# Key norms from the diagonal of k kᵀ, and triangular substitution on GpSimd, in a gated delta-rule block

## The chip, the cores and the metric

One core of one Trainium2 chip. The metric is the device time of one execution in microseconds (us); the median of three runs is compared.

## The reference, cut to what matters

The program is one adaptive-layernorm block: a linear-attention layer with a gated delta rule, then a sparse feed-forward layer, for 8 sequences of 256 tokens and 256 channels. For each of 16 key heads (two value heads each) the attention computes, over tokens t:

```python
q = _l2norm(qkv_c[..., :QD].reshape(Bq, Tq, NK, DK))
k = _l2norm(qkv_c[..., QD:2 * QD].reshape(Bq, Tq, NK, DK))
def step(S, inp):
    Sk = jnp.einsum('bhi,bhipj->bhpj', k_t, S)
    dv = b_t[..., None] * (v_t - Sk)
    upd = jnp.einsum('bhi,bhpj->bhipj', k_t, dv)
    S = S * d_t[:, :, None, :, None] + upd
    o = jnp.einsum('bhi,bhipj->bhpj', q_t, S)
```

`qkv_c` is a projection followed by a causal convolution over four tokens. The kernel does not step through tokens. It takes chunks of 128 tokens and solves, for each, a triangular system of 128 x 128 whose matrix holds the products k kᵀ scaled by decays, betas and the squared norms of the keys.

## The kernel before, in words

All of it is float32. Sequences go in pairs (`bp`, four pairs), key heads in groups of four (`kh`, `GH = 4`), so there are 16 groups and 64 combinations of pair and head. A head has two sequences x two chunks (`NCH = 2`) x two value heads, eight triangular systems; a group has 32, and each is cut into four diagonal blocks of 32 x 32 (`Q = 32`), 128 blocks in all, one per partition.

While a group is attended to, the next one is made ready (`ahead`), in these steps.

- `stage_a`, once per head: project the keys (`ps_k`, L432), convolve them (ScalarE L418, VectorE L420) into `k_t`. `norms2` then transposes `k_t` on TensorE (`ps_n2k`, L447, four transposes) and lets ScalarE square and sum each of the four pieces (L451, `junk`). From the squared norms VectorE makes `rk2` (L505) and `bk` (L507), and GpSimd the tile `diag` (L516) and `nk` (L523). TensorE forms k kᵀ (`ps_kk`, L532), VectorE runs a scan with decays over `diag` (`e`, L551; L547 in the first group) and multiplies `ps_kk` with `e` into `a_t` (L563). Four DMAs on the SP queue store the diagonal blocks to `scr` (L572).
- `stage_b`, once per group: load the 128 blocks (`blk`, L585), write the diagonal (GpSimd memset, L587), and invert them all at once by substitution, 30 steps of two VectorE instructions, a product into `tmp` (L604) and a subtraction from `blk` (L610). A step handles j x (31 - j) elements per partition, 30 to 240. After half of the steps and again at the end `turn` has ScalarE write negated copies (L592, L597); at the end they are stored to `scr_x` and `scr_y`.
- `levels`, once per head: load pieces of those inverses (`x_even`, `moved`, `x_top`, `low_up`) and join them on TensorE to 64 x 64 and then 128 x 128 (`ps_w`, `ps_t`, from L709 on).

Attention proper works on one head at a time: `prepare` makes q, v and the output gate (`cv`, `gz`), `attend` applies the inverses and ends with the output's norm on GpSimd (`rs`, a power, L105) and the gating on VectorE (`og`, L873), and `shares` multiplies with the output weights (`ps_y`, L903). Feed-forward and input normalisation of other sequences run in between (`feed_forward`, `fill`).

Generators are interleaved by `along`, which also paces the next group's preparation. The final order on every engine is made by the framework's scheduler at build time from its own estimate of durations; each engine then runs its instructions strictly in that order. PSUM is split in three pools: `ps_in` (three banks), `ps_inv` (two, with `ps_kk`, the levels and feed-forward) and `ps_mix` (three). In the first group no attention is there to run beside: `first_solved` holds the first heads' attention behind the substitution.

Of the kernel before, what the change touches and what calls it, by code (L numbers as in the profile page):

```python
# [11 lines left out]
F32 = mybir.dt.float32  # L12
AF = mybir.ActivationFunctionType
ALU = mybir.AluOpType
AX = mybir.AxisListType
# [3 lines left out]
P = 128  # L19
# [29 lines left out]
def adaln_block(  # L49
# [18 lines left out]
    nc = tc.nc  # L68
# [4 lines left out]
    NCH = T // P  # L73
    NK = w_heads.shape[0]
    NV = 2 * NK
    NS = 2 * NCH
# [6 lines left out]
    small = ctx.enter_context(tc.tile_pool(name="small", bufs=4))  # L83
    dram = ctx.enter_context(tc.tile_pool(name="dram", bufs=2, space=DRAM))
    ps_in = ctx.enter_context(tc.tile_pool(name="ps_in", bufs=3, space=PSUM))
    ps_inv = ctx.enter_context(tc.tile_pool(name="ps_inv", bufs=2, space=PSUM))
    ps_mix = ctx.enter_context(tc.tile_pool(name="ps_mix", bufs=3, space=PSUM))

    def bank(pool, shape, name):
        return pool.tile(shape, F32, tag=pool.name, name=name)  # L90
# [5 lines left out]
    ident = identx[:, 1:PE1]  # L96
# [269 lines left out]
    with ExitStack() as scope:  # L366
        rec_pool = scope.enter_context(tc.tile_pool(name="rec", bufs=7))
# [73 lines left out]
        def norms2(src, name):  # L441

            n2 = small.tile([P, 2, NCH], F32, tag=name, name=name)
            ps = bank(ps_in if name == "n2k" else ps_in, [P, 2, NCH, P], f"ps_{name}")
            for i in range(2):
                for n in range(NCH):
                    nc.tensor.transpose(ps[:, i, n, :], src[:, i, n * P : (n + 1) * P], ident)  # L447
            for i in range(2):
                for n in range(NCH):
                    junk = mixp.tile([P, P], F32, tag="junk", name="junk", bufs=2)  # L450
                    nc.scalar.activation(  # L451
                        junk, ps[:, i, n, :], AF.Square, accum_out=n2[:, i, n : n + 1]
                    )
            return n2
# [24 lines left out]
        def stage_a(kh, bp, hp, wk, h_bp, scr):  # L479

            rec = {"kh": kh, "bp": bp, "hp": hp, "h": h_bp}
            first = bp == 0 and kh < GH
            if not first:
                dbc = single.tile([P, 2, NS * PE1], F32, tag="dbc", name="dbc")
                nc.sync.dma_start(
                    out=dbc,
                    in_=d_dram[bp][kh]
# [3 lines left out]
            k_t = rec_pool.tile([P, 2, T], F32, tag="k_t", name="k_t")  # L491
# [4 lines left out]
            else:  # L496
                convolved(k_t, ps, conv_sb[:, kh, 0, :])
            yield rec
            n2 = norms2(k_t, "n2k")
            nc.vector.tensor_scalar_max(n2, n2, L2_EPS2)  # L500
            nk = small.tile([P, 2 * NCH], F32, tag="nk", name="nk", bufs=7)
            rec["nk"] = nk
# [5 lines left out]
                out=bk,  # L508
                in0=beta[bp][:, :, 2 * kh : 2 * kh + 2],
                in1=rk2[:, :, None].to_broadcast([P, 2 * NCH, 2]),  # L510
                op=ALU.mult,
# [13 lines left out]

            e = rec_pool.tile([P, 2, NS, PE1], F32, tag="e", name="e")
            rec["e"] = e
            ps_kk = bank(ps_inv, [P, 2 * NCH, P], "ps_kk")
            for i in range(2):
                for n in range(NCH):  # L530
                    kc = k_t[:, i, n * P : (n + 1) * P]
                    nc.tensor.matmul(ps_kk[:, i * NCH + n, :], lhsT=kc, rhs=kc, start=True, stop=True)  # L532
            if first:
                e_f, diag_f = e.rearrange("p i s t -> p (i s t)"), diag.rearrange("p s t -> p (s t)")
                for c0 in range(0, 2 * NS, 3):
# [21 lines left out]
                    ALU.add,  # L557
                )
            yield rec
            a_t = rec_pool.tile([P, 2, NS, P], F32, tag="a_t", name="a_t", bufs=6)  # L560
            rec["a"] = a_t
            for i in range(2):
                nc.vector.tensor_tensor(  # L563
                    out=a_t[:, i].rearrange("p (n h) t -> p n h t", h=2),
                    in0=ps_kk[:, i * NCH : (i + 1) * NCH, None, :].to_broadcast([P, NCH, 2, P]),
                    in1=e[:, i, :, 0:P].rearrange("p (n h) t -> p n h t", h=2),
                    op=ALU.mult,
                )
            a_f = a_t.rearrange("p i s t -> p (i s) t")
            scr_v = scr.rearrange("(g s q) a b -> g q a s b", g=GH, q=NQ)  # L570
            for q in range(NQ):
# [5 lines left out]
        def stage_b(scr, scr_x, scr_y):  # L577

            blk = single.tile([P, Q, Q], F32, tag="blk", name="blk")
            nc.sync.dma_start(out=blk, in_=scr)  # L585
            xb = single.tile([P, Q, Q], F32, tag="xb", name="xb")
            nc.gpsimd.memset(blk.rearrange("p a b -> p (a b)")[:, :: Q + 1], -1.0)  # L587
            yield

            def turn(rows):  # L590

                nc.scalar.activation(  # L592
                    xb[:, rows], blk[:, :, rows].rearrange("p b a -> p a b"), AF.Copy, scale=-1.0
                )
                if rows.stop == Q:
                    nc.sync.dma_start(out=scr_x, in_=xb)
                nc.scalar.activation(blk[:, :, rows], blk[:, :, rows], AF.Copy, scale=-1.0)  # L597
                if rows.stop == Q:
                    nc.sync.dma_start(out=scr_y, in_=blk)

            for j in range(1, Q - 1):
                m = Q - 1 - j
                tmp = single.tile([P, j, m], F32, tag="tmp", name="tmp", bufs=2)
                nc.vector.tensor_tensor(  # L604
                    out=tmp,
                    in0=blk[:, j, None, j + 1 :].to_broadcast([P, j, m]),
                    in1=blk[:, 0:j, j, None].to_broadcast([P, j, m]),
                    op=ALU.mult,
                )
                solved = nc.vector.tensor_tensor(  # L610
                    out=blk[:, 0:j, j + 1 :], in0=blk[:, 0:j, j + 1 :], in1=tmp, op=ALU.subtract
                )
                yield solved.ins
                if j == Q // 2:
                    turn(slice(0, Q // 2))
            turn(slice(Q // 2, Q))
            yield
# [599 lines left out]
```

## Time and profile before

| | |
|---|---|
| median of three runs | 2112.94 us (2111.67 to 2115.77) |
| profiled execution | 2109.53 us, span 2107.7 us |
| mean granted TensorE clock | 0.992 |
| DMA packets | 231.10 MB, mean 110 GB/s |

A row of the groups reads: line, engine, operation, output<-inputs, form x count | busy us in all, mean ns of one | idle time of the engine just before them and what ended most of it. A row of the timeline reads: start us, duration us, engine, line, operation, and in brackets the idle time before it. PE is TensorE, DVE VectorE, ACT ScalarE, POOL GpSimd, SPq the DMA queue of SyncE. TensorE shows two records for one float32 product and one for a transpose; the ends of its records are modelled.

### The profile page before, as it was taken

The page shows a single profiled execution, that of the slowest core. Times are in us where ns is not written, and L with a number is a line of the kernel's source. Part 1 is how long each engine was busy: PE and PEld are TensorE (multiplying, and loading weights), DVE is VectorE, ACT ScalarE, POOL GpSimd, SP SyncE. Part 2 cuts the span into 40 slices and gives each one's busy share as a digit, 9 for nine tenths or more (in the row PEclk, how much of TensorE's full clock was granted, in tenths as well). Part 3 has the DMA queues.
Part 4 walks back from the last instruction along what each step waited for, and adds up shares of the span by engine and source line. Part 5 has one row for each costly group of instructions (what it writes and reads, how often), then busy time and mean ns, then how long its engine had stood idle before and what let it go on. Part 6 is the DMA issues. An engine that isn't in the chain of part 4 may idle for free.

```text
span 2107.7 us, 46922 instructions
## 1 busy us (share of the span) xinstructions
PE 2027.1 (96%) x16684; PEld 1592.2 (76%) x16684; DVE 1683.9 (80%) x4103; ACT 1314.1 (62%) x4516; POOL 368.5 (17%) x375
## 2 busy tenths in 40 slices
PE   8989999999999999999999999999999999999998
PEld 5567777777778777787777778777777877778887
DVE  6788786887889797888878788897878978788557
ACT  3567676766756666576666656667565656657652
POOL 3111312112020211213021121211202021121010
PEclk9999999999999999999999999999999999999999
DMA  4352424324343443533433454343434343343236
GB/s 134 85 131 68 117 61 108 97 71 112 82 124 97 127 113 95 141 108 106 141 87 105 112 136 117 102 116 100 124 102 122 99 125 106 102 122 107 72 92 218
DMA packets 363434, 231.10 MB, mean 110 GB/s; under 512 B 293433, under 2 KB 305081, under 8 KB 363201
## 3 DMA queue, kind: packets, MB, share of 16 engines
q1 hardware_dynamic: 343328, 167.56, 30.6%
q10 hardware_dynamic: 19872, 60.54, 9.1%
q8 instruction: 133, 2.18, 0.4%
q14 instruction: 101, 0.82, 0.1%
HBM read 188.38 MB, written 29.12 MB: 103 GB/s over the span
## 4 chain that ended last, share of the span: by engine, by line
PE 49%; DVE 25%; ACT 8%; DMA 7%; issue 6%; POOL 4%; SPq 2%; ACTq 0%; DVEq 0%; POOLq 0%
PE ps_qv L432 7%; PE ps_y L903 6%; PE ps_z L646 6%; DVE cv L420 5%; PE ps_ks L814 3%; PE ps_k L432 3%; PE ps_ff L190 3%; POOL diag L516 3%; DVE a_t L563 2%; DVE e L551 2%; DVE tmp L604 2%; DVE blk L610 2%; PE ps_out L244 2%; PE ps_o L855 2%; DVE og L873 2%
## 5 line engine op out<-in xcount | busy, mean ns | idle before, releaser
L420 DVE SCALAR_TENSOR_TENSOR cv<-ps_qv,conv_sb,cv 128x510 f32<-128x510 f32 (+2 forms) x564 | 408.2, 738 | 76.0 <-ACT cv L418 72.1
L432 PE MATMUL ps_qv<-h_bp,wh 128*128 128x512 f32 x768 | 362.8, 600 | 5.0 <-DVE cv L420 4.7
L105 POOL TENSOR_TENSOR rs<-ss,minus_halves 128x4 f32<-128x4 f32 x128 | 133.1, 1045 | 987.4 <-DVE ss L860 976.7
L646 PE MATMUL ps_z<-wh,h_bp 128*128 128x256 f32 x1024 | 255.2, 388 | 14.7 <-DVE cv L420 14.4
L903 PE MATMUL ps_y<-wo,og_p 128*128 128x256 f32 x1024 | 238.6, 381 | 1.9 <-ACT gz L653 1.4
L840 ACT ACTIVATE junk<-o 128x128 f32<-128x128 f32 x512 | 154.1, 303 | 136.8 <-DVE o L856 119.3
L432 PEld LDWEIGHTS ps_qv<-h_bp,wh 128*128 128x128 f32 x768 | 134.5, 192 | 114.8 <-issue 101.5
L646 PEld LDWEIGHTS ps_z<-wh,h_bp 128*128 128x128 f32 x1024 | 186.2, 194 | 43.2 <-DVE cv L420 18.6
L903 PEld LDWEIGHTS ps_y<-wo,og_p 128*128 128x128 f32 x1024 | 188.3, 191 | 28.4 <-issue 4.3
L604 DVE TENSOR_TENSOR tmp<-blk 128x30 f32<-128x30 f32 (+14 forms) x480 | 157.3, 328 | 47.7 <-DMA blk<-scr 39.1
L418 ACT ACTIVATE cv<-ps_qv,conv_sb 128x512 f32<-128x512 f32 x188 | 129.5, 690 | 100.4 <-PE ps_qv L432 99.9
L516 POOL TENSOR_TENSOR diag<-consts,bk 128x1032 f32<-128x1032 f32 x64 | 122.8, 1919 | 343.4 <-DVE bk L507 327.1
L551 DVE TENSOR_TENSOR_SCAN e<-dbc,diag 128x1032 f32<-128x1032 f32 x60 | 138.2, 2304 | 35.4 <-POOL diag L516 30.9
L610 DVE TENSOR_TENSOR blk<-blk,tmp 128x30 f32<-128x30 f32 (+14 forms) x480 | 157.4, 328 | 11.2
L420 DVE SCALAR_TENSOR_TENSOR k_t<-ps_k,conv_sb,k_t 128x510 f32<-128x510 f32 (+1 forms) x189 | 139.7, 741 | 26.4 <-ACT k_t L418 23.0
L873 DVE SCALAR_TENSOR_TENSOR og<-o,rs,gz 128x128 f32<-128x128 f32 x512 | 147.2, 348 | 12.4 <-POOL rs L105 10.6
L814 PE MATMUL ps_ks<-u,cross 128*128 128x128 f32 x1024 | 143.8, 280 | 1.9 <-ACT u L808 1.3
L780 ACT ACTIVATE vn<-ps_v,nk 128x256 f32<-128x256 f32 x256 | 105.7, 481 | 49.2 <-PE ps_v L775 48.9
L190 PE MATMUL ps_ff<-h,w_ff 128*128 128x128 f32 x1024 | 130.5, 277 | 3.3 <-ACT h L149 2.4
L814 PEld LDWEIGHTS ps_ks<-u,cross 128*128 128x128 f32 x1024 | 128.1, 191 | 6.9 <-ACT u L808 2.6
L190 PEld LDWEIGHTS ps_ff<-h,w_ff 128*128 128x128 f32 x1024 | 123.0, 192 | 12.0 <-issue 5.1
L432 PE MATMUL ps_k<-h_bp,wk 128*128 128x512 f32 x256 | 126.1, 613 | 2.0 <-ACT junk L451 1.2
(180 smaller groups left out, 4273.0 us busy)
## 6 DMA issues: line engine op xcount, KB each, us to landing
wh<-in_w_heads ACTq DMA_DIRECT2D x64, 640.0 KB, 4.4
w_ff<-in_w_ff SPq DMA_DIRECT2D x128, 256.0 KB, 3.1
dbc<-d_dram SPq DMA_DIRECT2D x60, 516.0 KB, 3.8
wo<-in_w_heads ACTq DMA_DIRECT2D x32, 512.0 KB, 3.8
w_dn<-in_w_down SPq DMA_DIRECT2D x64, 256.0 KB, 2.8
wk<-in_w_keys SPq DMA_DIRECT2D x16, 512.0 KB, 4.5
scr<-a_t SPq DMA_DIRECT2D x256, 32.0 KB, 2.2
blk<-scr SPq DMA_DIRECT2D x16, 512.0 KB, 4.1
```

The source lines that it names most:

```text
L190: nc.tensor.matmul(ps[:, a, l, :], lhsT=w[:, k, l, :], rhs=h2[:, k, :], start=(k == 0), stop=(k == CC - 1),)
L420: nc.vector.scalar_tensor_tensor(out=dst[:, :, d:], in0=ps[:, :, : T - d], scalar=taps[:, KC - 1 - d : KC - d], in1=dst[:, :, d:], op0=ALU ...
L432: nc.tensor.matmul(ps.rearrange("p b t -> p (b t)"), lhsT=w[k], rhs=h_bp[:, k, :], start=(k == 0), stop=(k == CC - 1),)
L516: done = nc.gpsimd.tensor_tensor(out=diag, in0=identx[:, None, :].to_broadcast([P, 2 * NS, PE1]), in1=bk.rearrange("p n h -> p (n h)")[:, ...
L551: nc.vector.tensor_tensor_scan(e.rearrange("p i s t -> p (i s t)"), dbc.rearrange("p i f -> p (i f)"), diag.rearrange("p s t -> p (s t)"), ...
L604: nc.vector.tensor_tensor(out=tmp, in0=blk[:, j, None, j + 1 :].to_broadcast([P, j, m]), in1=blk[:, 0:j, j, None].to_broadcast([P, j, m]), ...
L610: solved = nc.vector.tensor_tensor(out=blk[:, 0:j, j + 1 :], in0=blk[:, 0:j, j + 1 :], in1=tmp, op=ALU.subtract)
L646: nc.tensor.matmul(ps[:, n, :], lhsT=h_bp[:, k, i * T + n * P : i * T + (n + 1) * P], rhs=wh[:, k * 640 + 384 : (k + 1) * 640], start=(k = ...
L814: nc.tensor.matmul(ps_ks[:, ct, h, :], lhsT=cross[:, h, ct, :], rhs=u0[:, h, :], start=True, stop=True)
L840: nc.scalar.activation(junk, o[:, n, h, :], AF.Square, accum_out=ss[:, n, h : h + 1])
L873: nc.vector.scalar_tensor_tensor(out=og[:, n, h, :], in0=o[:, n, h, :], scalar=rs[:, 2 * n + h : 2 * n + h + 1], in1=gz[:, i, n, h, :], op ...
L903: nc.tensor.matmul(ps_y[:, n, :], lhsT=og_p[:, j // 2, i, n, j % 2, :], rhs=wo[:, j // 2, j % 2, :], start=(j == 0), stop=(j == 3),)
```

## The change

The squared norms of the keys are no longer made by transposing and squaring. k kᵀ is formed before them, ScalarE copies it to SBUF (into one half of `a_t`), VectorE multiplies it with the identity into the other half and sums along the rows. The products with `e` read the SBUF copy. And the 60 instructions of the substitution are issued on GpSimd instead of VectorE. Lines after the first hunk are up to 16 higher than before, L510 and L513 are the new product and sum, L609 and L615 the substitution.

```diff
@@ stage_a
-            n2 = norms2(k_t, "n2k")
+            ps_kk = bank(ps_inv, [P, 2 * NCH, P], "ps_kk")
+            for i in range(2):
+                for n in range(NCH):
+                    kc = k_t[:, i, n * P : (n + 1) * P]
+                    nc.tensor.matmul(ps_kk[:, i * NCH + n, :], lhsT=kc, rhs=kc, start=True, stop=True)
+            a_t = rec_pool.tile([P, 2, NS, P], F32, tag="a_t", name="a_t", bufs=6)
+            rec["a"] = a_t
+            a_h = a_t.rearrange("p i (n h) t -> p (i n) h t", h=2)
+            kk, diagonal = a_h[:, :, 1], a_h[:, :, 0]
+            nc.scalar.copy(kk, ps_kk)
+            n2 = small.tile([P, 2, NCH], F32, tag="n2k", name="n2k")
+            nc.vector.tensor_tensor(
+                out=diagonal, in0=kk, in1=ident[:, None, :].to_broadcast([P, 2 * NCH, P]), op=ALU.mult
+            )
+            nc.vector.tensor_reduce(
+                out=n2.rearrange("p i n -> p (i n)"), in_=diagonal, axis=AX.X, op=ALU.add
+            )
             nc.vector.tensor_scalar_max(n2, n2, L2_EPS2)
...
-            ps_kk = bank(ps_inv, [P, 2 * NCH, P], "ps_kk")
-            for i in range(2):
-                for n in range(NCH):
-                    kc = k_t[:, i, n * P : (n + 1) * P]
-                    nc.tensor.matmul(ps_kk[:, i * NCH + n, :], lhsT=kc, rhs=kc, start=True, stop=True)
...
-            a_t = rec_pool.tile([P, 2, NS, P], F32, tag="a_t", name="a_t", bufs=6)
-            rec["a"] = a_t
-            for i in range(2):
-                nc.vector.tensor_tensor(
-                    out=a_t[:, i].rearrange("p (n h) t -> p n h t", h=2),
-                    in0=ps_kk[:, i * NCH : (i + 1) * NCH, None, :].to_broadcast([P, NCH, 2, P]),
-                    in1=e[:, i, :, 0:P].rearrange("p (n h) t -> p n h t", h=2),
-                    op=ALU.mult,
-                )
+            e_h = e[:, :, :, 0:P].rearrange("p i (n h) t -> p (i n) h t", h=2)
+            for h in range(2):
+                nc.vector.tensor_tensor(out=a_h[:, :, h], in0=kk, in1=e_h[:, :, h], op=ALU.mult)
@@ stage_b
             for j in range(1, Q - 1):
                 m = Q - 1 - j
                 tmp = single.tile([P, j, m], F32, tag="tmp", name="tmp", bufs=2)
-                nc.vector.tensor_tensor(
+                nc.gpsimd.tensor_tensor(
                     out=tmp,
                     in0=blk[:, j, None, j + 1 :].to_broadcast([P, j, m]),
                     in1=blk[:, 0:j, j, None].to_broadcast([P, j, m]),
                     op=ALU.mult,
                 )
-                solved = nc.vector.tensor_tensor(
+                solved = nc.gpsimd.tensor_tensor(
                     out=blk[:, 0:j, j + 1 :], in0=blk[:, 0:j, j + 1 :], in1=tmp, op=ALU.subtract
                 )
```

## The prediction

> **What bounds the kernel now.** I read the page's header and chain first, then the groups by form, then stretches of the timeline, then the busy times by window.
>
> ```profile
> span 2107.7 us, 46922 instructions
> PE 2027.1 (96%) x16684; PEld 1592.2 (76%) x16684; DVE 1683.9 (80%) x4103; ACT 1314.1 (62%) x4516; POOL 368.5 (17%) x375
> PE 49%; DVE 25%; ACT 8%; DMA 7%; issue 6%; POOL 4%; SPq 2%; ACTq 0%; DVEq 0%; POOLq 0%
> ```
>
> TensorE is busy nearly always, and half of the chain that ended last is its own work. A quarter is VectorE. So work taken off TensorE should count almost in full, and work taken off VectorE only where TensorE waits for it. The windows of one group of heads (the substitution runs from 885 to 927) say how much that can be:
>
> ```profile
> core 0: us, PE busy (x) PEld busy (x) DVE busy (x) ACT busy (x) POOL busy (x), PEclk, DMA share, GB/s
> 885.00:927.00 42.00, 40.51 (x328) 33.19 (x327) 39.67 (x123) 25.47 (x88) 5.81 (x8) 1.00 0.39 115
> 927.00:1009.00 82.00, 80.63 (x699) 62.95 (x698) 63.64 (x126) 53.13 (x190) 16.23 (x14) 1.00 0.42 112
> ```
>
> While the substitution is on it VectorE is full (39.67 of 42 us), yet TensorE idles only 1.5 us there. A free VectorE can win no more than that, some 15 to 20 us over all groups. The granted clock is 1.00, so it plays no part.
>
> The substitution itself is a chain of 60 dependent steps, and TensorE comes for its result:
>
> ```profile
> 885.55 0.16 POOL L587 MEMSET blk<- 128x32 f32 x1 [13.13 <-DMA blk<-scr]
> ...
> 926.67 0.21 DVE L610 TENSOR_TENSOR blk<-blk,tmp 128x30 f32<-128x30 f32 x1
> 926.91 1.11 ACT L592 ACTIVATE xb<-blk 128x512 f32<-128x512 f32 x1 [0.54 <-DVE blk L610]
> 928.05 0.32 SPq L596 DMA_DIRECT2D scr_x<-xb  x1
> 930.68 1.76 SPq L692 DMA_DIRECT2D x_even<-scr_x  x4
> 933.39 0.21 PE L709 MATMUL ps_w<-x_even,a_t 32*32 32x32 f32 x1
> ```
>
> blk lands at 885.5, the last step ends at 926.9, and 6.5 us later TensorE starts the next group's first level, about the moment x_even lands. There is almost no slack behind this chain. It is 41 us long because VectorE does other work between its steps. This decides the case.
>
> **TensorE, part by part.** The four transposes of L447 for the key norm go (64 heads, 256 transposes). The four products k k^T stay and only move ahead. What a head's transposes occupy is read from start to start, since the modelled ends overlap:
>
> ```profile
> 92.18 0.66 PE L447 MATMUL ps_n2k<-consts,k_t 128*128 128x128 f32 x4
> 92.67 1.05 PE L532 MATMUL ps_kk<-k_t 128*128 128x128 f32 x8
> ```
>
> That is 0.49 us; elsewhere 0.43 to 0.49. I take 0.46 x 64 = **-29 us** (27 to 31), in full, because nothing else fills TensorE's place.
>
> **ScalarE, VectorE and GpSimd.** The rows that price these:
>
> ```profile
> L451 ACT ACTIVATE junk<-ps_n2k 128x128 f32<-128x128 f32 x256 | 69.3, 293 | 33.7 <-PE ps_n2k L447 32.9
> L563 DVE TENSOR_TENSOR a_t<-ps_kk,e 128x512 f32<-128x512 f32 x128 | 82.0, 682 | 0.2
> L516 POOL TENSOR_TENSOR diag<-consts,bk 128x1032 f32<-128x1032 f32 x64 | 122.8, 1919 | 343.4 <-DVE bk L507 327.1 <-DVE mv L132 10.0 <-DVE rstd L134 6.3
> L1014 POOL TENSOR_TENSOR taps<-consts,conv_sb 128x512 f32<-128x512 f32 x1 | 1.0, 1041 | 4.6 <-DMA conv_sb<-in_conv_w 4.6
> L657 POOL TENSOR_SCALAR eps_q<-n2q 128x4 f32<-128x4 f32 x64 | 23.8, 373 | 40.4 <-ACT junk L451 36.7
> ```
>
> ScalarE loses 256 squares (69.3 us) and their accumulator reads (56.7 us), and gains 64 copies of 128x512 at 0.60 us (the copy raw, L466): 39 us. Net -87 us, off the path.
>
> VectorE loses both substitution groups (157.3 and 157.4 us) and gains a masking product and a sum per head. For both I take the 128x512 row of L563, 0.68 us (a sum reads one operand less; L131, 256 elements with one input, costs 0.42 us as products of 256 do). 64 x 1.36 = 87 us. The two a_t products keep their size. Net -228 us: VectorE falls to about 1456 us (69%). Outside the substitution windows it rises from 64 to about 69 of 82 us, still with room. The new steps lie on the way from k to diag, but that way runs a whole group ahead. They also free the ps_kk bank after the copy rather than after a_t. I book 0 for all of this, between -10 us (TensorE's idle time in the substitution windows above) and +10 us (5.4 us more VectorE work per group outside them; should an eighth of it reach the path, 15 x 0.7).
>
> GpSimd gains 960 dependent products. Two rows of its products give 1.69 ns per element ((1919 - 1041) / 520) and 0.18 us fixed. The 30 shapes average 165 elements: 0.28 + 0.18 = 0.46 us. The steps wait for one another; from the end of bk (L507) to the start of diag, GpSimd takes 0.14 us to wake. Bounds per step: 0.46 us (no waking) and 0.79 us (the fixed part of L657, 0.37, with 0.14). I take 0.46 + 0.14 = **0.59 us**, since the products' own line is nearer than another instruction's. VectorE's step was 0.33 us.
>
> **First group.** Nothing interleaves there: VectorE's chain took 23.2 us (59.8 to 83.0), and TensorE started the first level at 90.0, when x_even had just landed. On GpSimd it is 60 x 0.59 + 2 rstd at 0.65 + one eps_q = 37 us, 14 us longer. The changed kernel as built has two more ps_k projections ahead of that level (4 products of 0.86 us = 3.4 us), so **+10.5 us** (+3 at 0.46 us, +23 at 0.79).
>
> **The other 15 groups.** GpSimd's queue runs in order. In the changed kernel as built, some four rs (L105, 1.05 us each) and two eps_q stand between the chain's steps, behind each rs the og of VectorE, and behind the chain's end ScalarE's xb with the attention's copies queued after it; on SP the stores of scr_x and scr_y wait for that xb as they do now, with x_even, moved and w_ff behind them. Chain: 35.4 + 4.2 + 0.7 = 40.3 us. VectorE and GpSimd also block each other:
>
> ```profile
> 124.41 1.92 POOL L516 TENSOR_TENSOR diag<-consts,bk 128x1032 f32<-128x1032 f32 x1
> 124.79 2.47 DVE L873 SCALAR_TENSOR_TENSOR og<-o,rs,gz 128x128 f32<-128x128 f32 x4
> ```
>
> Four og take 1.12 us elsewhere (at 159.35); here the first had to wait for diag to end. No VectorE instruction with two SBUF operands gets through while diag runs, whereas cv and aq, with one operand in PSUM, keep their 0.74 and 0.68 us. About 30 such instructions fall into one substitution window. Each waits at most for the running step: 30 x 0.25 = 7.5 us of VectorE per group, covered by the 20 us it gives up there. In the other direction the trace shows little: diag took 1.95 instead of 1.92 us where VectorE had begun first. That gives 30 x 0.03 = 1 us; if GpSimd had to sit out a whole og (0.35 us) less its waking time, 30 x 0.21 = 6 us. I add 3: **43.5 us**.
>
> The allowance: adding up TensorE's rows, the built order places about 86 us of TensorE work between a group's last ps_k and the first level, where it was 78. But k k^T of the fourth head stands about 5 us later than its transposes did, and copy, product and sum take 1.5 us more than the squares. So some 1.5 us is left on top of 41.3: **43 us**. The chain is 0.5 us late per group, 15 x 0.5 = **+8 us**.
>
> Sum against the profiled execution (2109.5 us, span 2107.7): 2109.5 - 29 + 10.5 + 8 = 2099. The median of the runs (2112.9) lies 3.4 us above that execution, so 2102.
>
> **Two rules of the Trainium skill speak against the change.** "GPSIMD Engine Reference", section Performance versus the Vector engine, gives about 2.6 cycles per element at 1.2 GHz for a product of two tensors, and tells one to use VectorE; the rows here have 1.69 ns. As an estimate by that page a step is 0.08 us dearer (165 elements), a chain 4.8 us, and the time would be near 2180 us. "SBUF — State Buffer", section Who interferes with whom, says that the later of the two engines waits for the other's whole instruction; the og row agrees for VectorE, the 0.03 us of diag does not for GpSimd. As an estimate by that page the chain loses the 6 us per group rather than 3, and the time would be near 2147 us.
>
> **Rivals.**
> - *The chain on GpSimd comes late in every group* and takes the place of TensorE's transposes. For it: x_even lands just in time today, and short strided rows were never run on GpSimd here. Against: the two product rows lie on one line, and the built order leaves more room. Without lateness the change wins 18.5 us; over 15 groups that is gone at 1.2 us late, a step of 0.61 us. At 0.65 us: 39 + 4.9 + 3 = 46.9, 3.9 us late, 59 us, and 14 us at the start: 2109.5 - 29 + 14 + 59 = 2153 (2157 as median). At 0.70 us about 2205. Slower.
> - *TensorE's saved time is eaten by waits of the same size*, so that nothing shows. For it: busy spans are modelled, the chain gives TensorE only 49%. Against: start to start, products follow each other without gaps. 2109 to 2117 as median.
> - *The relief is larger*: the step is near 0.46 us, no group is late, VectorE's freed time ends TensorE's waits. 2109.5 - 29 + 3 - 10 = 2074, median 2077.
>
> **Chances.** Forecast (2090 to 2108) 0.38, larger relief 0.14, no difference 0.12, late chain 0.36. A fifth of a per cent, 4 us, is about what a measurement of this kernel can tell from no change. The range reaches down to the larger relief (2077) and up to a step of 0.65 us (2157), leaving out the dearest steps.
>
> **What would show it.** Right: TensorE 29 us less busy; L615 on GpSimd starting every 0.59 us; the last L615 ending 41 to 45 us after the memset of blk; the first L714 not idle for x_even. Wrong: ScalarE's xb waiting for L615 in most groups, TensorE idle behind x_even, VectorE's og waiting for rs, or steps above 0.65 us.

## The result, and the profile after

The changed kernel takes 2200.9 us (median of four runs, 2195.1 to 2205.2) against 2112.8 us: ratio 1.0413, 95% interval 1.0386 to 1.0440, so 87 us slower. The prediction said 2102, with a range up to 2157. The profiled execution took 2205.2 us with a span of 2203.3.

First the head of the page: span, busy times with their share of the span, and the shares of the chain that ended last.

```profile
span 2203.3 us, 46030 instructions
PE 2047.4 (93%) x16428; PEld 1598.4 (73%) x16428; DVE 1565.2 (71%) x3271; ACT 1279.1 (58%) x4069; POOL 886.2 (40%) x1335
...
PE 10%; DVE 4%; POOL 3%; DMA 2%; ACT 1%; issue 1%; SPq 0%; DVEq 0%; ACTq 0%; POOLq 0%
```

The 256 transposes are gone (16684 records became 16428), yet TensorE is busy 20 us longer, and its idle time, span less busy time, nearly doubled: 2107.7 - 2027.1 = 80.6 us before, 155.9 now. The busy time grew because of the clock. Its mean is 0.974 (0.992 before); the stretches at half speed cost TensorE 56.3 us of full-speed time within the span, before 17.1. TensorE was busy for 104.1 us of these stretches, before for 32.8. Counting that at half, its work at full speed fell from 2010.7 to 1995.3 us, so the transposes did leave some 15 us less to do. Idle time (75 us more) and half clock (36 us more) ate that several times over. Between the first 55 and the last 20 us of the span, TensorE idled for 2 us or more 26 times, 78.9 us in all; before it did so twice, 4.4 us. Those few long stalls are about as long as the whole growth of its idle time. The chain now explains only a fifth of the span and no longer names a culprit, so the waits have to be read.

The table by stretch, one substitution and the rest of its group (columns as in the prediction's table: length, busy us of the engines, granted clock, DMA share, GB/s):

```profile
925.90:968.60 42.70, 39.67 (x249) 30.81 (x246) 26.27 (x58) 22.38 (x78) 35.97 (x68) 0.96 0.26 79
968.60:1057.20 88.60, 85.20 (x773) 66.96 (x772) 68.59 (x135) 56.02 (x181) 17.13 (x15) 0.98 0.47 124
```

VectorE has its free time (it is busy for 26.27 of 42.70 us), and TensorE gets nothing from it: it stands 3.0 us in the substitution, where it stood 1.5. The rest of the group, 82 us in the table before, takes 88.6.

The substitution's own timeline in that group, from the landing of `blk` to TensorE's first level:

```profile
925.88 0.16 POOL L592 MEMSET blk<- 128x32 f32 x1 [16.52 <-DMA blk<-scr]
...
968.38 0.27 POOL L615 TENSOR_TENSOR blk<-blk,tmp 128x30 f32<-128x30 f32 x1
968.68 1.11 ACT L597 ACTIVATE xb<-blk 128x512 f32<-128x512 f32 x1 [1.82 <-POOL blk L615]
...
972.84 1.74 SPq L697 DMA_DIRECT2D x_even<-scr_x  x4
...
975.35 0.21 PE L714 MATMUL ps_w<-x_even,a_t 32*32 32x32 f32 x1
```

42.8 us against 41 before, and TensorE starts the level without having stood for `x_even`. The substitution is not late here. What is late stands in the lists of waits (the waiting instruction, what it waited for: us in all, times, longest), here the rows of VectorE, TensorE and its weight loads:

```profile
DVE og L878 <- POOL rs L105: 60.5, 28, 6.9
PE ps_u L811 <- DVE aq L801: 29.0, 13, 5.2
PE ps_ks L819 <- DVE aq L801: 19.8, 9, 3.4
PEld ps_w L714 <- DMA x_even<-scr_x: 16.9, 11, 4.7
```

Before, these four were 10.6, 5.1, 0.6 and 3.4 us. Of the 26 long stalls 13, with 38.8 of the 78.9 us, waited for `aq`. One such stall in the timeline, merged from VectorE, GpSimd and TensorE:

```profile
1053.31 0.16 DVE L865 SCALAR_TENSOR_TENSOR ss<-ss,eps_q 128x4 f32<-128x4 f32 x1 [0.82 <-ACT junk L845]
...
1057.20 0.15 POOL L592 MEMSET blk<- 128x32 f32 x1 [17.03 <-DMA blk<-scr]
...
1059.06 0.36 POOL L615 TENSOR_TENSOR blk<-blk,tmp 128x84 f32<-128x84 f32 x1
1059.38 1.01 POOL L105 TENSOR_TENSOR rs<-ss,minus_halves 128x4 f32<-128x4 f32 x1
...
1060.43 1.94 DVE L878 SCALAR_TENSOR_TENSOR og<-o,rs,gz 128x128 f32<-128x128 f32 x4 [5.17 <-POOL rs L105]
...
1068.06 0.68 DVE L801 TENSOR_TENSOR aq<-ps_kq,e 128x512 f32<-128x512 f32 x1
1068.79 1.01 PE L811 MATMUL ps_u<-vn,t_inv 128*128 128x128 f32 x3 [5.24 <-DVE aq L801]
```

`ss`, the input of `rs`, is there at 1053.5. In GpSimd's order `rs` stands behind the memset, which waits for `blk` to land, and behind six instructions of the substitution; it starts 5.9 us later (3.7 us of the load, 2.2 of the six instructions). VectorE, in order too, stands 5.17 us at `og`, then catches up with what had piled up, and `aq`, which TensorE needs, comes out 5.24 us late. The table by stretch shows what the clock makes of it (the granted clock is the first number behind the busy times):

```profile
1055.00:1060.00 5.00, 5.00 (x38) 2.92 (x37) 0.26 (x1) 4.52 (x21) 2.40 (x8) 1.00 0.55 181
...
1065.00:1070.00 5.00, 1.21 (x5) 1.21 (x6) 5.00 (x11) 0.00 (x0) 4.32 (x9) 0.69 0.00 0
1070.00:1075.00 5.00, 5.00 (x39) 4.63 (x38) 4.90 (x11) 3.03 (x12) 4.45 (x8) 0.63 0.01 3
```

At full load after the stall TensorE has a mean clock of 0.63. This stall is paid for twice: once idle, once at half speed.

### The profile page after: what moved, and what is told of

Same layout as the page of the kernel before. It is cut to its first block, busy times and chain, and to the rows that moved or that the text cites. A ratio compares the mean times of both kernels' runs of the same rounds, so it can differ in the third digit from the quotient of the medians.

```text
span 2203.3 us, 46030 instructions
## 1 busy us (share of the span) xinstructions
PE 2047.4 (93%) x16428; PEld 1598.4 (73%) x16428; DVE 1565.2 (71%) x3271; ACT 1279.1 (58%) x4069; POOL 886.2 (40%) x1335
## 5 line engine op out<-in xcount | busy, mean ns | idle before, releaser
L432 PE MATMUL ps_qv<-h_bp,wh 128*128 128x512 f32 x768 | 371.7, 611 | 0.9 <-DVE y L919 0.9
L105 POOL TENSOR_TENSOR rs<-ss,minus_halves 128x4 f32<-128x4 f32 x128 | 141.9, 1113 | 434.0 <-DVE ss L865 415.6
L651 PE MATMUL ps_z<-wh,h_bp 128*128 128x256 f32 x1024 | 260.1, 393 | 13.5 <-DVE cv L420 13.3
L615 POOL TENSOR_TENSOR blk<-blk,tmp 128x30 f32<-128x30 f32 (+14 forms) x480 | 253.9, 529 | 36.1
L609 POOL TENSOR_TENSOR tmp<-blk 128x30 f32<-128x30 f32 (+14 forms) x480 | 238.5, 497 | 33.4
L878 DVE SCALAR_TENSOR_TENSOR og<-o,rs,gz 128x128 f32<-128x128 f32 x512 | 187.7, 426 | 61.6 <-POOL rs L105 60.5
L819 PE MATMUL ps_ks<-u,cross 128*128 128x128 f32 x1024 | 149.6, 288 | 24.8 <-DVE aq L801 19.8
L819 PEld LDWEIGHTS ps_ks<-u,cross 128*128 128x128 f32 x1024 | 133.1, 198 | 41.4 <-DVE aq L801 21.6
L190 PE MATMUL ps_ff<-h,w_ff 128*128 128x128 f32 x1024 | 135.5, 281 | 13.1 <-DMA w_ff<-in_w_ff 9.9
L861 DVE TENSOR_TENSOR o<-o,ps_o 128x256 f32<-128x256 f32 x128 | 52.5, 414 | 107.5 <-PE ps_o L860 100.3
```

The source lines that it names most:

```text
L105: nc.gpsimd.tensor_tensor(out=out, in0=in_, in1=minus_halves[:, :n], op=ALU.pow)
L190: nc.tensor.matmul(ps[:, a, l, :], lhsT=w[:, k, l, :], rhs=h2[:, k, :], start=(k == 0), stop=(k == CC - 1),)
L432: nc.tensor.matmul(ps.rearrange("p b t -> p (b t)"), lhsT=w[k], rhs=h_bp[:, k, :], start=(k == 0), stop=(k == CC - 1),)
L609: nc.gpsimd.tensor_tensor(out=tmp, in0=blk[:, j, None, j + 1 :].to_broadcast([P, j, m]), in1=blk[:, 0:j, j, None].to_broadcast([P, j, m]), ...
L615: solved = nc.gpsimd.tensor_tensor(out=blk[:, 0:j, j + 1 :], in0=blk[:, 0:j, j + 1 :], in1=tmp, op=ALU.subtract)
L651: nc.tensor.matmul(ps[:, n, :], lhsT=h_bp[:, k, i * T + n * P : i * T + (n + 1) * P], rhs=wh[:, k * 640 + 384 : (k + 1) * 640], start=(k = ...
```

## The experiments

My theory after the result: in-order queues that the change rearranged make a few instructions late on every engine (for the substitution's half, `rs` behind it on GpSimd), and a stretch of half clock follows most long stalls of TensorE. The rivals: the substitution's result itself is late; the engines slow each other down in SBUF; or any other written order than that of the kernel before would lose as much. "Cost" below is (ratio - 1) x 2112.8 us, each kernel against runs of the kernel before on the same chip; the changed kernel's is +87.

| run | what it is | median us | ratio, 95% | cost us |
|---|---|---|---|---|
| e1 | new norms, substitution on VectorE | 2181.5 | 1.0306 to 1.0343 | +68 |
| e2 | old norms, substitution on GpSimd | 2181.3 | 1.0304 to 1.0345 | +69 |
| e3 | changed, `rs` on VectorE | 2183.1 | 1.0288 to 1.0349 | +67 |
| e4 | e1, `rs` on VectorE | 2191.3 | 1.0347 to 1.0390 | +78 |
| e5 | before, a third scratch buffer | 2124.7 | 1.0038 to 1.0079 | +12 |
| e6 | e2, `rs` on VectorE | 2136.8 | 1.0084 to 1.0143 | +24 |
| e7 | e1 without the diagonal | 2163.2 | 1.0201 to 1.0257 | +48 |
| e8 | changed, first substitution on VectorE | 2197.3 | 1.0346 to 1.0419 | +81 |
| e9 | e1, k kᵀ read in PSUM, no copy | 2155.5 | 1.0171 to 1.0220 | +41 |
| e10 | before, k kᵀ early and copied | 2169.0 | 1.0230 to 1.0277 | +54 |
| e11 | before, k kᵀ copied | 2148.2 | 1.0117 to 1.0200 | +33 |
| e12 | before, k kᵀ early | 2122.9 | 1.0025 to 1.0062 | +9 |
| e13 | e9, first group with old norms | 2133.0 | 1.0076 to 1.0114 | +20 |
| e14 | changed, first group as before | 2183.2 | 1.0307 to 1.0354 | +70 |
| e15 | all mends together | 2126.2 | 1.0037 to 1.0079 | +12 |
| e16 | before, norms by a column of ones | 2166.7 | 1.0229 to 1.0281 | +54 |
| e17 | before, a copy that nobody reads | 2112.4 | 1.0021 to 1.0046 | +7 |
| e18 | e11 with a tile of its own | 2124.3 | 1.0079 to 1.0113 | +20 |

### The two halves, and the scale of the output's norm (e1 to e4)

e1, against the changed kernel:

```diff
-                nc.gpsimd.tensor_tensor(out=tmp, ...)
-                solved = nc.gpsimd.tensor_tensor(...)
+                nc.vector.tensor_tensor(out=tmp, ...)
+                solved = nc.vector.tensor_tensor(...)
```

> The changed kernel with the 960 substitution instructions put back on VectorE; only the norms from the diagonal are new. If all of the loss comes from the substitution on GpSimd (queue, lateness or port), the 256 transposes saved on TensorE show: 2113 - 29 = 2084 us, with 10 us either way, and og (L878) waits for rs about as little as in the kernel before (11 us). If the norms themselves are what costs (VectorE's extra product and sum, the later k k^T), this kernel lies above 2113 us, up to 2200.

e2 is the kernel before with only the last hunk of the change, the substitution on GpSimd.

> The kernel before with the substitution on GpSimd and the old norms. If the substitution is all of the loss: 2201 + 29 = 2230 us, between 2200 and 2240, with og waiting for rs 50 us or more. If the norms are the loss: about 2113 us.

e3 is the changed kernel, e4 is e1, both with a reciprocal in place of the power -1/2 (so the scale has other values; e6 and e15 below have it too):

```diff
-            rsqrt(rs, ss.rearrange("p n h -> p (n h)"))
+            nc.vector.reciprocal(rs, ss.rearrange("p n h -> p (n h)"))
```

> The changed kernel, but the norm of the output (rs) is a reciprocal on VectorE in place of the power -1/2 on GpSimd, so that no rs stands in GpSimd's queue (the values differ by that; it costs VectorE 128 x 0.17 = 22 us and takes 142 us from GpSimd). Queue theory (rs waits behind the substitution's steps and the load of blk, og holds up VectorE behind it): more than half of the loss goes, 2150 us or less, and no wait of og for rs is left. Result theory (the inverses come late; ScalarE's xb and x_even): 2185 to 2205 us, xb still waits 40 us or more. Port theory (VectorE and GpSimd block each other): 2185 to 2205 us, og still 0.42 us instead of 0.35.

> Control for the run before it: substitution on VectorE, new norms, and the same reciprocal on VectorE. Under every theory it lies within 8 us of the kernel with the new norms alone, since rs on GpSimd made og wait only 11 us in the kernel before. If it is faster by much more, moving rs is a gain of its own and the run with rs on VectorE has to be read against this one.

Each half alone costs about 69 us (2181.5 and 2181.3), both together 87: they are not additive, and the norms, which I had booked at a gain, are half of it. e2 shows the stall of the changed kernel in its plain form: in its trace TensorE stands longer than 0.6 us at `ps_u` for `aq` 11 times, 41.7 us in all, up to 5.5 us each, most of them in the same place of a group, with VectorE 3.7 to 4.9 us at `og` for `rs` ahead of them. One of them, merged from VectorE, GpSimd and TensorE; here six substitution steps alone stand between `ss` and `rs`:

```profile
791.53 0.42 DVE L860 SCALAR_TENSOR_TENSOR ss<-ss,eps_q 128x4 f32<-128x4 f32 x1
...
795.23 0.65 POOL L610 TENSOR_TENSOR blk<-blk,tmp 128x220 f32<-128x220 f32 x1
795.84 1.01 POOL L105 TENSOR_TENSOR rs<-ss,minus_halves 128x4 f32<-128x4 f32 x1
...
796.88 2.31 DVE L873 SCALAR_TENSOR_TENSOR og<-o,rs,gz 128x128 f32<-128x128 f32 x4 [4.93 <-POOL rs L105]
...
804.22 0.67 DVE L796 TENSOR_TENSOR aq<-ps_kq,e 128x512 f32<-128x512 f32 x1
804.94 1.22 PE L806 MATMUL ps_u<-vn,t_inv 128*128 128x128 f32 x4 [5.39 <-DVE aq L796]
```

But taking `rs` off GpSimd gave only 20 us in the changed kernel (e3), where I had expected 50 or more, while the same edit in e4 cost 10, where I had allowed 8. So there was more than the queue ahead of `rs`.

### Is any other order as bad? And `rs` without the new norms (e5, e6)

e5 changes one number of the kernel before:

```diff
-                    junk = mixp.tile([P, P], F32, tag="junk", name="junk", bufs=2)
+                    junk = mixp.tile([P, P], F32, tag="junk", name="junk", bufs=3)
```

> The kernel before with one number changed: the scratch of the squared norms (tag junk) gets three buffers and not two. Every instruction stays, none gets longer; but the order that is written for each engine is made from estimated durations, and it comes out different in hundreds of places on TensorE. Theory A (both halves of the change cost about 70 us because any other order than that of the kernel before leaves TensorE short gaps, and the granted clock falls after them): 2150 to 2190 us. Theory B (each half costs its 70 us by its own waits): within 12 us of the kernel before, 2100 to 2125 us.

> The kernel before with the substitution on GpSimd (old squared norms), and the scale rs as a reciprocal on VectorE and not as a power on GpSimd (the scale has other values for it). With the substitution alone on GpSimd, TensorE stood 41.7 us in 11 gaps, each for aq, and in front of each aq VectorE had stood 3.7 to 4.9 us at og for rs, which is queued on GpSimd behind the substitution; with the half clock after each gap that is about 70 us. Theory 1 (the queue in front of rs is this half's whole loss): 2105 to 2130 us. Theory 2 (VectorE slowed by GpSimd's use of SBUF, or any other order): 2160 us or more.

e5: 2124.7, 12 us, with hundreds of instructions in other places of TensorE's order. So another order can cost 12 us by itself. One control is no bound on what an order can cost; I read a cost of 12 us or less as not to be told from order, and one of 30 or more as likely to have a cause of its own. e6: 2136.8, between the ranges of its two theories; of the substitution's 69 us, 45 go when `rs` no longer stands behind it. TensorE's stalls at `ps_u` for `aq` over 0.6 us fall from 41.7 to 18.5 us, and the half-clock loss from 55 to 17 us. That shows the queue ahead of `rs` as the main loss of this half; what the other 24 us are stays open.

### Where the norms lose (e7, e9 to e12, e17, e18)

e7 leaves the diagonal out of e1:

```diff
-            nc.vector.tensor_tensor(out=diagonal, in0=kk, in1=ident..., op=ALU.mult)
-            nc.vector.tensor_reduce(out=n2, in_=diagonal, axis=AX.X, op=ALU.add)
-            nc.vector.tensor_scalar_max(n2, n2, L2_EPS2)
+            nc.vector.tensor_reduce(out=n2, in_=kk[:, :, 0:8], axis=AX.X, op=ALU.max)
+            nc.vector.tensor_scalar_max(n2, n2, 300.0)
```

> New norms with the substitution on VectorE, as in the run of the norms alone (2181 us), but without the product with the identity and its sum: the squared norm is the largest of eight columns of the copy of k k^T, held to 300 or more, so the values are others. That leaves out 1.4 us of VectorE per head (about 90 us in all) and keeps the early k k^T, its copy on ScalarE and the product of the decays from SBUF. Theory V (VectorE's 1.5 us in a row in front of aq and x_top is the loss): 2090 to 2115 us. Theory P (the place of k k^T, the copy, the buffers, or the order): 2160 us or more.

2163.2: without VectorE's 1.5 us per head 20 of the 68 us go; 48 remain. The next four separate early place, copy and transposes. e9 is e1 with

```diff
-            nc.scalar.copy(kk, ps_kk)
-                out=diagonal, in0=kk, in1=ident...
+                out=diagonal, in0=ps_kk, in1=ident...
```

and the old product of `ps_kk` with `e`.

> New norms from the diagonal, substitution on VectorE, but k k^T is not copied to SBUF: the product with the identity and the old product of the decays both read PSUM. Against the run of the norms alone (2181 us) ScalarE loses 64 copies, and the decays' product has one operand in SBUF and not two; k k^T still stands early, and its bank is held from there to the decays' product. Theory C (the copy and the product from SBUF are the loss): 2080 to 2115 us. Theory E (the early place of k k^T is the loss): 2150 to 2190. Theory T (the transposes and their squares on ScalarE are what paced this part; without them the order is worse): 2140 to 2185.

e10 is the kernel before with these lines ahead of its norms, and the decays' product from `kk`; e11 has them in the old place behind the norms; e12 has only the matmuls ahead of the norms.

```diff
+            ps_kk = bank(ps_inv, [P, 2 * NCH, P], "ps_kk")      # and its four matmuls
+            a_t = rec_pool.tile([P, 2, NS, P], F32, tag="a_t", name="a_t", bufs=6)
+            kk = a_t.rearrange("p i (n h) t -> p (i n) h t", h=2)[:, :, 1]
+            nc.scalar.copy(kk, ps_kk)
             n2 = norms2(k_t, "n2k")
```

> The kernel before with its old norms (transposes and squares), substitution on VectorE; k k^T moved ahead of the norms and copied by ScalarE into the tile of A, and the decays' product from SBUF, as the change has them. Against the kernel before that is a copy of 0.6 us per head more. Theories C and E: 2140 to 2180 us. Theory T: 2110 to 2130.

> As the last, but k k^T stays in its old place, behind the norms: only the copy, the product of the decays from SBUF and the earlier taking of the tile of A are new. Theory C: 2140 to 2180 us. Theories E and T: 2110 to 2130.

> The kernel before with one thing moved: the four matmuls of k k^T stand ahead of the old norms and not behind them; nothing is copied, and the bank is held longer. Theory E: 2140 to 2190 us. Theories C and T: 2105 to 2130.

The early place alone costs 9 us (e12, 2122.9), the copy alone 33 (e11, 2148.2), both 54 (e10, 2169.0); with the new norms and no copy it is 41 (e9, 2155.5) instead of 68. No one of the three theories fits all four: e9 lies above the range of C, e12 below that of E, and e10 and e11 above that of T. The copy's route is the dearest part, and with the old norms still in place. And the transposes, once gone, pay next to nothing: from e10 to e7, which has no transposes and squares and in their place a small maximum on VectorE, the cost falls by 6 us, not by 29, with overlapping intervals. TensorE's work at full speed, counted as above, does fall there, from 2022.0 to 1986.9 us; its idle time (113.5 to 127.0) and its half clock take most of it back.

What in the copy? e17 keeps it and reads nothing of it; e18 gives it a tile of its own, so that the tile of A is taken late again:

```diff
+            spare = mixp.tile([P, 2 * NCH, P], F32, tag="spare", name="spare", bufs=2)
+            nc.scalar.copy(spare, ps_kk)
```

> The kernel before and one thing more: behind k k^T in its old place, ScalarE copies the bank to a spare tile that nobody reads; the decays' product reads PSUM as before. If ScalarE's 64 copies of some 0.6 us, in the order of its queue, are what cost 32 us in the run with k k^T copied (2148): 2138 to 2158 us. If it is the product from SBUF or the tile of A: 2110 to 2128.

> As the run with k k^T copied in its old place (2148 us), but the copy goes to a tile of its own, and the tile of A is taken at the decays' product as in the kernel before. If the early tile of A cost the 32 us: 2110 to 2128 us. If the copy or the product from SBUF did: 2138 to 2158.

ScalarE's 64 copies cost 7 us (e17, 2112.4 against 2106.8 on that chip), not 33. With the product reading SBUF it is 20 us (e18, 2124.3, in the range that I gave for the early tile as the cause), and with the tile taken early 33 (e11). The product from SBUF has two operands there and is blocked by GpSimd's `diag`, as the prediction saw for `og`: in the changed kernel nine of 128 take 1.4 to 2.3 us, each begun while `diag` runs and ended 0.5 us after it. Its mean is 762 ns where the product from PSUM took 682, only 10 us over 128 instructions. No wait in the trace of e11 shows what the early tile does. The steps from 7 to 20 to 33 are each about as large as another order's 12 us, so I leave them unexplained.

### The first group (e8, e13, e14)

e8 gives only the first group's substitution back to VectorE.

> The changed kernel with the first group's substitution on VectorE, the fifteen others on GpSimd. The first group's chain took 36.4 us on GpSimd against 23 us on VectorE, with nothing else to do beside it, and the changed kernel was some 32 us behind at the end of its second group. If that start is a loss of its own, 2201 - 13 - 10 = 2178 us, 2170 to 2188; if another loss takes its place, 2195 to 2205 us.

2197.3, 6 us less, with overlapping intervals: though its chain takes 36.4 us instead of 23, it is hardly the start's loss. e13 is e9 with a branch, e14 the changed kernel with the same branch and the first substitution on VectorE:

```diff
+            if first:
+                n2 = norms2(k_t, "n2k")          # and k k^T behind them, as before
+            else:
                 ...                              # k k^T, its diagonal
```

> As the norms from PSUM (2155 us), but the first group's four heads keep the old norms, with k k^T behind them. In the trace of the norms from PSUM the start of the second group's substitution was 34 us late, and the end 41.5 us. Theory S (the loss is the first group's start, where nothing else fills TensorE): 2155 - 34 = 2121, 2108 to 2132 us. Theory G (every group pays): 2140 us or more.

> The changed kernel with the first group as in the kernel before: old norms, and substitution on VectorE; the fifteen others unchanged. In the changed kernel the second group's substitution began 31.9 us late, in the run with only the first substitution on VectorE 22.5 us late. Theory S: 2201 - 25 = 2176 us, 2165 to 2185. If another loss takes its place, as in the run with only the first substitution on VectorE (2197): 2190 us or more.

e13 (2133.0, a little above what I expected) takes 21 us off e9, e14 (2183.2) 17 us off the changed kernel: the new norms lose in the first group, where nothing else fills TensorE. (e14 also has the first substitution on VectorE, for which e8 gave 6 us.) The table by stretch from 30 to 60 us, first e9, then e13:

```profile
30.00:60.00 30.00, 21.48 (x94) 17.03 (x93) 22.05 (x40) 0.93 (x3) 11.50 (x8) 0.69 0.22 48
```

```profile
30.00:60.00 30.00, 29.32 (x164) 20.45 (x163) 19.04 (x42) 8.30 (x36) 11.41 (x9) 0.99 0.47 126
```

8 us of TensorE and a clock of 0.69 are lost in those 30 us. In e9, where k kᵀ keeps its bank until the decays' product, the timeline names the wait, the two banks of `ps_inv` for four heads:

```profile
38.06 2.08 PE L503 MATMUL ps_kk<-k_t 128*128 128x128 f32 x8 [4.48 <-DVE a_t L571]
48.82 2.05 PE L503 MATMUL ps_kk<-k_t 128*128 128x128 f32 x8 [2.72 <-DVE a_t L571]
```

In the changed kernel the copy frees the bank; there the same stretch has TensorE busy 25.3 us at a clock of 0.77, and its long wait (3.44 us, at 49.6) is for VectorE's scan `e`.

### All mends together (e15), and a cheaper norm (e16)

e15 puts e13, the substitution on GpSimd in the other groups, and `rs` on VectorE together.

> All mends together on the changed kernel: first group as in the kernel before; in the others norms from PSUM without the copy, substitution on GpSimd, rs as a reciprocal on VectorE (other values of the scale). If the losses found are the whole, what is left is the 24 us of the substitution with rs on VectorE and some 5 to 10 of the norms: 2112 + 24 + 8 = 2144 us, 2120 to 2155. If a loss of the two halves together is still unnamed: 2165 us or more.

2126.2 us, +12: the mends take 75 of the 87 us away, and what is left is no more than another order cost in e5. Against e13 (+20) the substitution on GpSimd is then no loss at all, though e6 had kept 24 us with it. That also tests the rivals: in 15 of 16 groups GpSimd carries the same substitution beside VectorE as in the changed kernel (though the products with `e` read PSUM again), so neither its late result nor SBUF is the large loss. TensorE's work at full speed is 23 us below that of the kernel before (1987.5 against 2010.7); its idle time (25 us more) and its half clock (14 us more) still outweigh that.

With GpSimd's and ScalarE's work cheap and TensorE's dear, I tried a norm without transposes and without VectorE, in the kernel before:

```diff
-                    nc.tensor.transpose(ps[:, i, n, :], src[:, i, n * P : (n + 1) * P], ident)
-                    nc.scalar.activation(junk, ps[:, i, n, :], AF.Square, accum_out=n2[:, i, n : n + 1])
+            nc.scalar.activation(sq, src, AF.Square)
+                    nc.tensor.matmul(ps[:, i, n : n + 1], lhsT=sq[:, i, n * P : (n + 1) * P], rhs=ones, ...)
```

> The kernel before (substitution on VectorE, k k^T in its old place), but both squared norms, of keys and of queries, come from one square of 128x512 on ScalarE and four matmuls against a column of ones; the limit and the product for the queries read PSUM on VectorE. Of the kernel before that removes 512 transposes (0.115 us each when they follow closely), and 512 squares with their reads of the sum, 249 us of ScalarE; it adds 128 activations of 0.69 us and 512 matmuls of one column, for which the trace has no row; their weight load is that of a transposed block at least. VectorE gains 64 operations of some 0.16 us. If TensorE's time sets the pace and slack covers the rest: 2112 - 10 to - 35, 2077 to 2102 us. If the written order costs as much as in the run with a third scratch (13 us): 2090 to 2125.

A plain miss: +54 us. The groups (count, busy us, mean ns) say why:

```profile
L450 PEld LDWEIGHTS ps_n2k<-ones,sq 128*128 128x128 f32 x512 | 66.8, 195 | 5.2 <-ACT sq L446 1.5 <-issue 1.5
L450 PE MATMUL ps_n2k<-ones,sq 128*128 128x1 f32 x512 | 64.3, 242 | 0.7 <-ACT sq L446 0.7
```

256 products have 512 records, each with a load of 128 columns of weights, 195 ns, where a transpose has one record and a load of 141 (L447 in the kernel before). One column of output doesn't make it cheap: TensorE is 68 us busier than before, and its work at full speed is 58 us more. The record count was known from the kernel before and should have priced it.

No kernel here beats the one before.

## Why the prediction was wrong, point by point

**What held.** The first group's chain took 36.4 us (37 predicted), the next four 37 to 38, the others 41 to 44 (43.5 predicted for all fifteen). A step with its waking is 0.58 us ((36.4 - 1.5) / 60, leaving out the two `rstd` and the `eps_q`; 0.59 predicted). TensorE's weight loads stood for `x_even` 16.9 us in all, 13.5 more than before (8 predicted as lateness). The rival "the chain comes late in every group" had the right sign and the wrong mechanism; that its figure for a step of 0.70 us, about 2205, lies near the measured time is luck. The estimate from the Trainium skill, "GPSIMD Engine Reference", section Performance versus the Vector engine (near 2180 us), had the right sign too, but its dearer step did not show.

**"-29 us, in full, because nothing else fills TensorE's place" failed.** The work went (15 us in the changed kernel, 35 from e10 to e7), the time did not: e10 to e7 gave 6 us. Half of the chain being TensorE's own did not mean that each microsecond taken from it shortens the span. Each in-order engine has its next wait behind it, and 29 us over 64 heads are 0.46 us apiece, less than the waits that changed.

**"That way runs a whole group ahead ... I book 0" failed, and was the norms' half, +68 us.** By the runs, 27 of these go with the copy and the product from SBUF (e1 to e9), 21 with the first group (e9 to e13), and 20 are left (e13). The steps are early as data. But they are written into the same in-order queues as the attention's `aq`, `x_top` and `cv`. I had priced VectorE's sum of work (5.4 us more per group outside the substitution) and not what it stands in front of. In e7's trace TensorE waits 5.4 to 5.5 us for `aq` three times, while VectorE never stands still: two convolution steps, a product with `e`, a row of another sequence's normalisation and a scan of 2.29 us come first. The end of one such wait (the view names the 0.14 us instruction behind `aq`):

```profile
1129.72 2.29 DVE L559 TENSOR_TENSOR_SCAN e<-dbc,diag 128x1032 f32<-128x1032 f32 x1
1131.93 0.66 DVE L798 TENSOR_TENSOR aq<-ps_kq,e 128x512 f32<-128x512 f32 x1
1132.51 0.14 DVE L134 TENSOR_SCALAR rstd<-mv 128x1 f32<-128x1 f32 x1
...
1132.65 1.22 PE L808 MATMUL ps_u<-vn,t_inv 128*128 128x128 f32 x4 [5.48 <-DVE rstd L134]
```

All of these are instructions that the kernel before has too, in another order. That such queues are the norms' loss outside the first group is argued from waits like this one; no run takes them away alone, and the part of the copy stays open. In the first group the sentence was not even true: there is no group ahead of which to run, and e13 and e14 give 17 to 21 us for it.

**The only meeting point I looked at was `x_even`; it was `aq`.** The working has "four rs and two eps_q stand between the chain's steps, behind each rs the og of VectorE", and charges them to the chain (4.2 us). It never asked the reverse: how long `rs` waits for the chain. It listed "VectorE's og waiting for rs" as a sign of being wrong, and gave it no price. Measured: 60.5 us of waiting instead of 10.6, 45 us of time when it stands alone (e2 to e6), 20 in company of the norms (changed to e3).

**"+10.5 us" for the first group** had the right length of the chain; giving the chain back to VectorE gave 6 us (e8), not clear of noise. The larger loss of that group was the norms'.

**"The granted clock is 1.00, so it plays no part" failed.** It was 1.00 in the windows I looked at; behind its start the kernel before had no stall of over 2.4 us. With longer stalls the half clock took 39 us more (56.3 against 17.1). The trace before held the sign of it, nine stretches at half speed.

**"30 x 0.25 us of blocked VectorE, covered"** held in sum: `og` has a mean of 426 ns instead of 348, 40 us over 512, or 2.7 per group. The other direction was misread: in front of the two `diag` of 1.95 us VectorE had begun `xn`, with one tensor operand, not two. In the changed kernel a step lasts up to 0.82 us longer than in the first group where VectorE's instructions with two operands in SBUF had begun before it. That makes 14 us over the fifteen groups, 0.9 per group, where 3 were booked.

**"Net -228 us" for VectorE failed**, though its share of a longer span (71%) is near the 69% forecast: it fell by 119 us. Records of neighbouring instructions overlap. Without the 960 substitution rows, 315 us by their own sum, the busy time before would be 256 us less. The new product and sum add 82 us to the busy time (87 booked), and `og` and the products with `e` became longer. ScalarE likewise fell by 35 us, not by 87. As VectorE's free time was booked at 0, the forecast time does not depend on it.

## What to carry to other kernels

When an instruction chain moves to another engine, price both directions of its queue: not only what the chain waits for there, but each short instruction that is already on that engine, how long it now stands behind the chain, and who waits for it. A step that is early as data is still in the way of what is queued behind it; and work taken from a busy engine pays only as far as the next wait. On TensorE a stall of 2 us or more should be priced above its length: over the 20 profiles 245 of them lasted 717 us, and the half-speed stretches that began in them or soon after cost 461 us more, an estimate of 1.6 times their length.

## What the runs showed of the hardware

**Stalls and the half clock.** The granted clock here was either 1.00 or 0.50, the low stretches lasting nearly always 3.41 or 6.83 us. Over the 20 profiles of this case, leaving out the first 55 and the last 20 us, a low stretch began during an idle time of TensorE or within 3.6 us of its end:

| TensorE idle for | how many | followed by half clock |
|---|---|---|
| 0.6 to 1 us | 427 | 37 (9%) |
| 1 to 2 us | 420 | 78 (19%) |
| 2 to 2.5 us | 91 | 62 (68%) |
| 2.5 to 3.5 us | 104 | 85 (82%) |
| 3.5 us and more | 50 | 50 |

With 313 low stretches in 20 spans, any time of 4.5 us has one begin in it in 3% of cases by chance (an estimate). No run took a stall away without changing other things, so the link is a count and not a test. The Trainium skill, "TensorE: Matmul & The Clock Gate", section Part 1: The HAM clock gate, puts the clock at half after an idle window of about 3.4 us, with windows that run freely; the lengths of 3.41 and 6.83 us agree with that window, but here half clock followed stalls of 2 to 2.5 us two times in three.

**Waiting in order.** A GpSimd instruction of 1.01 us (`rs`) whose input was ready cost TensorE 5.2 us, because it stood behind a memset that waited for a DMA and behind six steps of 0.2 to 0.4 us.

**A one-column float32 product** on TensorE has two records with a weight load of 195 ns each, against one of 141 ns for a transpose: with 512 of them in place of 512 transposes TensorE was 68 us busier (e16).

**GpSimd and VectorE in SBUF.** Each made the other wait: a product of VectorE with two operands in SBUF took up to 2.29 us instead of 0.68 beside `diag`, and a step of GpSimd up to 0.82 us more behind such instructions of VectorE.
